# Padded pair scores, list flags on another engine, and an experts' first layer computed transposed, in an attention and mixture-of-experts kernel

## The chip, the cores and the metric

The kernel runs on one core of one Trainium2 chip. The metric is the device time of one execution in microseconds. Before the change it is 2405.32 us, the median of three runs (2403.5 to 2418.53). The profile was taken in an execution whose span, from the first to the last instruction, is 2203.7 us; positions in time below are microseconds from the start of that span.

## The reference, cut to what matters

One layer: graph attention over a sparse adjacency, then a mixture of 8 experts of which each token uses 2. There are 4096 tokens of 512 numbers, 8 heads of 64.

```python
def gnn(n, adj, Wks, Wqs, Wvs, Wo):
    adj = maximum(adj, eye)
    q, k, v = (einsum('nd,hdk->hnk', n, W) for W in (Wqs, Wks, Wvs))
    scores = einsum('hqk,hmk->hqm', q, k) * 64 ** -0.5
    scores = scores + 0.01 * eye - 1e16 * (1 - adj)
    return einsum('hqm,hmk,hko->qo', softmax(scores), v, Wo)

def ffn(x, Wg, bg, W1, b1, W2, b2):
    topk_scores, topk_idx = top_k(x @ Wg + bg, 2)
    h = gelu(einsum('nd,edh->neh', x, W1) + b1)      # 8 experts, 512 -> 512
    y = einsum('neh,ehf->nef', h, W2) + b2           # 512 -> 512
    return sum over the two chosen experts of softmax(topk_scores) * y

x = x + gnn(layernorm(x), adj, ...)
x = x + ffn(layernorm(x), ...)
```

The adjacency is 4096 x 4096 in float32, random, with many more entries among the first tokens than among the last.

## The kernel before

All matrix products are in float32; a float32 matmul is two records in the trace, a transpose is one. There are three stages.

**Stage one** (64 steps, in an order written by hand): keys, values and queries of all tokens are projected and stored in device memory. At the same time the adjacency is read in 32 pieces of 2 MB, one for each tile of 128 queries, and for each tile a list of the keys that any of its queries has is made. Keys that only the first 64 or only the last 64 queries of the tile need stand at the ends of the list, so that a chunk of 128 keys is "half" or full. Part of the making of lists is a comparison of slot numbers with the places at which each run of keys begins:

```python
def begun(i):
    for k, (t0, t1) in enumerate(ranges(i)):
        started[i, k] = lp.tile([P, (t1 - t0) * P], BF16, ...)
        nc.gpsimd.tensor_scalar(
            started[i, k], slots[:, t0 * P : t1 * P], base[g][:, k, j : j + 1], None,
            op0=ALU.is_ge)

def list_rows(i, k):                      # TensorE: started as weights, small matmuls
    ...
        nc.tensor.matmul(pr[:, t, :], started[i, q][:, s], row_x[g][:, r, j, :], ...)

load_at = {13 * i // 8: i for i in range(NT)}                       # step of each load
lists_from = {13 * (g * G + G - 1) // 8 + 3: g for g in range(NTB)}  # 4 tiles a group
...
    if u - 2 in load_at:
        neighbours(load_at[u - 2])        # VectorE: reduces a piece of the adjacency
```

**Attention**: for each tile of queries, its own 128 keys and then each chunk of its list (395 items in all; 229 of them are half, 166 full). An item's keys, values and mask are gathered from device memory by GpSimd. A step of the pipeline is:

```python
turn(n + 3)     # 8 transposes of 64-row blocks of the keys, 64 x 64, to PSUM pk
scores(n + 2)
values(n)       # 16 matmuls' records: weights 128 x 64 (values), 64 or 128 queries
later(n)        # pieces of the tile before: sums, rb, output product, routing
masked(n + 2)   # VectorE: e * mask

def scores(n):
    s = [ps_s.tile([P, NP, P], F32, ...) for r in range(2)]
    for p in range(NP):                   # 4 pairs of heads
        for r in range(2):                # the two heads of a pair, 64 rows each
            rows = slice(r * KD, (r + 1) * KD)
            nc.tensor.matmul(part(s[r], i, c)[:, p, :], k[rows, p, :],
                             q_in[i][rows, p, q], start=True, stop=True)
    for r in range(2):
        nc.scalar.activation(e[:, r * NP : (r + 1) * NP], part(s[r], i, c), AF.Exp)
```

Here `q` is 128 queries in a full item and 64 in a half one. During this stage the first layer's weights of all experts are loaded, 32 loads of 256 KB (`w1`). When it ends, the second layer's are loaded in 8 loads of 1 MB:

```python
w2 = w2p.tile([P, E, HC, D], F32, name="w2")
for e in range(E):
    nc.sync.dma_start(out=w2[:, e], in_=W2[e].rearrange("(c p) f -> p c f", p=P))
```

The routing writes each token's row, twice, to the place `xs_d` of its two experts, and a table says which expert and which place each of 71 tiles of 128 rows has.

**Experts**, 71 tiles, each with the weights of one expert:

```python
def turn(b):                              # 4 transposes of the rows to xT
def hidden(b):
    for c in range(DC):
        nc.tensor.matmul(ph, xTs[b][:, c, :], w1[:, bass.ds(es[b], 1), c, :], ...)
    nc.vector.tensor_add(h, ph, bs[b][:, 0])
    nc.scalar.activation(h, h, AF.Gelu)
def turn_hidden(b):                       # 4 transposes of h to PSUM pht
    ...
    nc.vector.tensor_copy(hT, pt)
def second(b):
    for c in range(HC):
        nc.tensor.matmul(py, hTs[b][:, c, :], w2[:, bass.ds(es[b], 1), c, :], ...)
    nc.vector.tensor_add(y, py, bs[b][:, 1])
    nc.scalar.mul(y, y, gate[:, 1:2])
    nc.gpsimd.indirect_dma_start(out=out, ..., in_=y, compute_op=ALU.add)

for b in range(NB):
    fetch(b + 4)                          # rows, b1 and b2 spread over 128 partitions
    turn_hidden(b); hidden(b + 1); turn(b + 2); second(b)
```

Of the kernel before, what the change touches and what calls it, by code (L numbers as in the profile page):

```python
# [20 lines left out]
P = 128  # L21
# [22 lines left out]
def kernel(  # L44
# [174 lines left out]
    def load_q(i):  # L219
        q_in[i] = qp.tile([P, NP, P], F32, tag="q", name=f"q_{i}")  # L220
        nc.sync.dma_start(out=q_in[i], in_=qT_d[:, :, ts(i, P)])
# [46 lines left out]
    with tc.tile_pool(name="wqkv", bufs=1) as wp, tc.tile_pool(name="p1", bufs=3) as work, tc.tile_pool(  # L268
# [39 lines left out]
        )  # L308

# [21 lines left out]
        def list_constants():  # L331
            nc.vector.tensor_sub(step, ident, step)
            nc.vector.tensor_mul(other, other, part)
            nc.vector.tensor_scalar(other, other, -1.0, 1.0, op0=ALU.mult, op1=ALU.add)
            nc.vector.memset(again_c, 1.0)
            nc.vector.memset(again_c[:, :, :, 0:1], 0.0)
            nc.vector.tensor_scalar_mul(corner, corner, -1.0)
            for k in range(KV // D):
                nc.sync.dma_start(out=kv_d[N : N + 1, ts(k, D)], in_=blank[:1, :D])
# [60 lines left out]
        def count_3(g):  # L400
# [24 lines left out]
            base[g] = b  # L425

        def steps(g):

# [3 lines left out]
            nc.tensor.matmul(  # L432
                pd[:, 1:], corner, x_g[:, :2], start=False, stop=True, skip_group_check=True
            )
            pe = ps_l.tile([P, G, NX], F32, tag="l", name=f"pe_{g}")
            nc.tensor.matmul(pe, step, x_g[:, 2], start=True, stop=True)
            dx = lp.tile([P, 4, G, NX], BF16, tag="dx", name=f"dx_{g}")
            nc.scalar.copy(dx[:, :3], pd)
            nc.scalar.copy(dx[:, 3], pe)
# [7 lines left out]
        def begun(i):  # L447

            g, j = divmod(i, G)
            for k, (t0, t1) in enumerate(ranges(i)):  # L450
                if t0 == t1:
# [5 lines left out]
                nc.gpsimd.tensor_scalar(  # L457
                    started[i, k], slots[:, t0 * P : t1 * P], base[g][:, k, j : j + 1], None,
                    op0=ALU.is_ge,
# [5 lines left out]
        def list_rows(i, k):  # L465
# [4 lines left out]
            for t in range(m):  # L470
                h = half_of(i, t0 + t)

                of = [(0, 0)] if h == 0 else [(2, 3)] if h == 1 else [(0, 0), (1, 1), (2, 2)]
# [8 lines left out]
        def list_keys(i, k):  # L482
# [21 lines left out]
            for h, u0, u1 in ((0, 0, a), (None, a, b), (1, b, listed[i])):  # L504
                u0, u1 = max(u0, t0), min(u1, t0 + m)
                if u0 < u1:
                    u = slice(at[i] + u0, at[i] + u1)
                    k = key[:, u0 - t0 : u1 - t0]
                    if h is None:
                        nc.vector.tensor_scalar_add(mask_of[:, u], k, float(i * (N + 1)))  # L510
                    else:
                        nc.vector.tensor_scalar(
# [27 lines left out]
        def lists_at(g, s):  # L540

            def rows(i):
                for k in range(len(chunks(i))):
                    list_rows(i, k)
                    if k:
                        list_keys(i, k - 1)
# [3 lines left out]
            if s == 0:  # L550
                count_1(g)
                return [lambda: count_2(g)]
            if s == 1:
                count_3(g)
                begun(i)
                return [lambda: steps(g)]
            if s == 2:
                begun(i + 1)
                return []
            if s == 3:  # L560
                return [lambda: rows(i)]
            if s == 4:
                keys(i)
                begun(i + 2)
                return [lambda: rows(i + 1)]
            if s == 5:
                keys(i + 1)
                begun(i + 3)
                return [lambda: rows(i + 2)]
            if s == 6:  # L570
                keys(i + 2)
                return [lambda: rows(i + 3)]
            keys(i + 3)
            return []
# [40 lines left out]
        def pack():  # L615
            i, c = ready.pop(0)
            m = work.tile([P, P], F32, tag="mask", bufs=6, name=f"pm_{i}_{c}")
# [5 lines left out]
        lists_from = {13 * (g * G + G - 1) // 8 + 3: g for g in range(NTB)}  # L623
        for u in range(8 * NTB + 1):
# [4 lines left out]
            for k in range(8):  # L629
                if u - k in lists_from:  # L630
                    due += lists_at(lists_from[u - k], k)
# [19 lines left out]
            if u - 2 in load_at:  # L651
                neighbours(load_at[u - 2])
                if load_at[u - 2] == NT - 1:
# [4 lines left out]
                    q_cm = tc.tile_pool(name="q", bufs=2, side="right")  # L658
                    qp = q_cm.__enter__()
                    load_q(0)  # L660
# [6 lines left out]
            if u - 8 in lists_from:  # L667
                g = lists_from[u - 8]
                ready += [
                    (i, c) for i in range(g * G, g * G + G) for c in range(listed[i])  # L670
                    if c % 5 in (1, 3)
                ]
# [29 lines left out]
    def route_1(m, l, pool, name):  # L702
# [4 lines left out]
        ahead = pool.tile([P, m, E, E], F32, tag="ahead", name=f"ahead_{name}")  # L707
        nc.vector.tensor_tensor(ahead, other, own, op=ALU.is_gt)
        same = pool.tile([P, m, E, E], F32, tag="same", name=f"same_{name}")
# [129 lines left out]
    w1_cm = tc.tile_pool(name="w1", bufs=1)  # L839
    w1p = w1_cm.__enter__()  # L840
    w1 = w1p.tile([P, E, DC, HID], F32, name="w1")
    GROUPS = [4] * (NT // 4 - 1) + [2, 1, 1]
    with tc.tile_pool(name="p2a", bufs=2) as two, tc.tile_pool(
# [38 lines left out]
        def load_x(i):  # L882
            x_in[i] = two.tile([P, D], F32, tag="xt", name=f"xr_{i}")
# [21 lines left out]
        def part(t, i, c):  # L905

            if half_of(i, c) is None:
                return t
            heads = t.shape[1]
            t = t.rearrange("p h q -> p (h q)")[:, : heads * QH]  # L910
            return t.rearrange("p (h q) -> p h q", h=heads)

        def scores(n):

            i, c = items[n]
            s = [ps_s.tile([P, NP, P], F32, tag="s", name=f"s{r}_{i}_{c}") for r in range(2)]
            k = kT.pop(n)
            q = queries(i, c)
            for p in range(NP):
                for r in range(2):  # L920
                    rows = slice(r * KD, (r + 1) * KD)
                    nc.tensor.matmul(  # L922
                        part(s[r], i, c)[:, p, :], k[rows, p, :], q_in[i][rows, p, q],
                        start=True, stop=True,
                    )
            if c < 0:
                e = two.tile([P, 2 * NP, P], F32, tag="acc", name=f"acc_{i}")
                acc[i] = e
            else:
                e = part(work.tile([P, 2 * NP, P], F32, tag="e", name=f"e_{i}_{c}"), i, c)  # L930
            for r in range(2):
                nc.scalar.activation(e[:, r * NP : (r + 1) * NP], part(s[r], i, c), AF.Exp)  # L932
            es[n] = e

# [8 lines left out]
        def values(n):  # L943
# [6 lines left out]
            for p in range(NP):  # L950
                for r in range(2):
                    h = 2 * p + r

                    nc.tensor.matmul(  # L954
                        po[i][r * KD : (r + 1) * KD, p, q], v[:, ts(h, KD)], e[:, r * NP + p, :],
                        start=(c < 0 and p == 0), stop=(c == listed[i] - 1),
                        skip_group_check=True,
                    )
# [10 lines left out]
        def piece(i, k):  # L969
# [3 lines left out]
            if k == 1:  # L973
                sums[i] = ps_e.tile([P, P], F32, tag="e", name=f"sums_{i}")
                a = acc.pop(i)
                for t in range(2):
                    for q in range(4):
# [3 lines left out]
                            a[:, r * NP + 2 * u + t, :], start=(t == 0), stop=(t == 1),  # L981
# [121 lines left out]
        loads = [(e, c) for e in range(E) for c in range(DC)]  # L1103
        for n, (i, c) in enumerate(items):
# [5 lines left out]
            if c == 2:  # L1110
                load_x(i)
            if n >= 56 and n % 7 == 0 and loads:
                e, d = loads.pop(0)
                nc.sync.dma_start(out=w1[:, e, d], in_=W1[e, ts(d, P), :])
            if c < 0 and i:
                osb[i - 1] = single.tile([P, NP, P], F32, tag="o", bufs=2, name=f"o_{i - 1}")
# [11 lines left out]
        osb[NT - 1] = single.tile([P, NP, P], F32, tag="o", bufs=2, name=f"o_{NT - 1}")  # L1128
        nc.scalar.copy(osb[NT - 1], po.pop(NT - 1))

# [3 lines left out]
        w2_cm = tc.tile_pool(name="w2", bufs=1, side="right")  # L1134
# [284 lines left out]
```

## Time and profile before

| what | value |
| --- | --- |
| time, median of 3 runs | 2405.32 us |
| span of the profiled execution | 2203.7 us |
| TensorE busy | 2040.5 us, 93% |
| VectorE busy | 1319.2 us, 60% |
| GpSimd busy | 1242.8 us, 56% |
| ScalarE busy | 870.1 us, 39% |
| moved by DMA | 481.71 MB, 219 GB/s over the span |
| mean granted TensorE clock | 0.949 of full |

In the profile, PE is the matmuls of TensorE and PEld its weight loads, DVE is VectorE, ACT ScalarE, POOL GpSimd and SP SyncE, whose queue issues most transfers. A group's line gives the line of the kernel, the engine, the operation, what it writes and reads, the count, and then the busy time and the mean duration of one in ns. The page cuts the span in 40 equal slices and prints one digit a slice: busy tenths for an engine, tenths of the full clock for PEclk, tenths of the 16 DMA engines' time for DMA. The timeline gives start, length, engine, line, operation and names; the ends of matmuls in it are modelled, while their starts are records. A wait is idle time of an engine just before an instruction, put down to what released it last.

### The profile page before, as it was taken

The numbers are of one execution on the slowest core, as the hardware profiler recorded it, in microseconds if no ns is written. First come the engines' busy times: TensorE is split into PE (matmuls) and PEld (weight loads), VectorE is DVE, ScalarE is ACT, GpSimd is POOL, SyncE is SP. The second block draws the span as 40 slices with busy tenths as digits, with TensorE's granted clock in tenths as the row PEclk, the third lists the DMA queues.
The fourth block names the chain that finished last, engine by engine and source line by source line (L and its number), as shares of the span: only waits on it lengthen the run. The fifth ranks groups of instructions, "written<-read, shape, count | busy, mean of one in ns | idle before, by whom it ended". The sixth has DMA issues, their size and how long they took to land. (4 is left out here: it accounts for less than half of the span.)

```text
span 2203.7 us, 52479 instructions
## 1 busy us (share of the span) xinstructions
PE 2040.5 (93%) x20620; PEld 1366.7 (62%) x20620; DVE 1319.2 (60%) x2387; ACT 870.1 (39%) x1842; POOL 1242.8 (56%) x1072
## 2 busy tenths in 40 slices
PE   7877879899999999999999999999829999999998
PEld 3333334348888888888788878777614444444444
DVE  4888586724887767777677777777723222333232
ACT  2121211124666646655556555656412222222222
POOL 1769888885888657678676766667412112111112
PEclk9988988896999989999999999999959999999999
DMA  7737787847788868878788878878475556555554
GB/s 281 301 127 234 258 294 261 263 120 236 247 260 273 273 216 275 281 239 282 247 268 266 267 249 248 264 234 252 165 257 127 134 131 136 136 134 140 137 136 96
DMA packets 215039, 481.71 MB, mean 219 GB/s; under 512 B 49618, under 2 KB 81874, under 8 KB 210692
## 3 DMA queue, kind: packets, MB, share of 16 engines
q0 software_dynamic: 79232, 242.18, 37.1%
q1 hardware_dynamic: 134404, 234.01, 33.7%
q8 instruction: 168, 2.75, 0.5%
q10 hardware_dynamic: 1152, 2.10, 0.3%
q14 instruction: 83, 0.68, 0.1%
HBM read 400.59 MB, written 77.58 MB: 217 GB/s over the span
## 5 line engine op out<-in xcount | busy, mean ns | idle before, releaser
L225 POOL DMA_INDIRECT kv<-kv_d,key_of x363 | 430.4, 1186 | 231.8 <-PE po L954 136.4
L941 DVE TENSOR_TENSOR e<-e,mask 128x512 f32<-128x512 f32 (+1 forms) x363 | 322.6, 889 | 204.0 <-ACT e L932 200.4
L922 PE MATMUL s<-q,kT 64*128 64x64 f32 (+1 forms) x5808 | 409.4, 282 | 2.7 <-ACT acc L932 2.7
L1354 POOL DMA_INDIRECT out_dram<-y,r x71 | 110.6, 1558 | 474.0 <-ACT h L1324 124.7
L922 PEld LDWEIGHTS s<-q,kT 64*128 64x128 f32 x5808 | 373.4, 196 | 2.9 <-ACT acc L932 2.9
L896 ACT COPY kT<-pk 128x512 f32<-128x512 f32 x395 | 232.1, 588 | 285.1 <-PE pk L893 277.3
L932 ACT ACTIVATE e<-s 128x256 f32<-128x256 f32 (+1 forms) x726 | 297.1, 461 | 101.5 <-PE s L922 98.6
L960 DVE TENSOR_TENSOR acc<-acc,e 128x512 f32<-128x512 f32 (+1 forms) x363 | 320.4, 883 | 1.4 <-PE po L954 1.4
L954 PE MATMUL po<-e,kv 128*64 128x64 f32 (+1 forms) x5808 | 311.3, 251 | 0.0
L225 POOL DMA_INDIRECT mask<-in_adjT_dram,mask_of x230 | 257.7, 1121 | 71.9 <-issue 50.0
L457 POOL TENSOR_SCALAR started<-slots,base 128x384 bf16<-128x384 int16 (+12 forms) x96 | 229.0, 2401 | 76.6 <-DVE longer L407 75.7
L954 PEld LDWEIGHTS po<-e,kv 128*64 128x64 f32 x5808 | 246.4, 141 | 34.7 <-issue 0.8
L1318 PE MATMUL ph<-w,xT 128*128 x568 | 258.3, 598 | 0.7 <-ACT xT L207 0.7
L1347 PE MATMUL py<-w,hT 128*128 x568 | 255.6, 593 | 0.9 <-DVE hT L1332 0.9
L352 DVE TENSOR_REDUCE flags<-adjT 128x64 f32<-128x4096 f32 x32 | 141.2, 4413 | 81.2 <-DMA adjT<-in_adjT_dram 81.2
L1352 DVE TENSOR_TENSOR y<-py,bb 128x512 f32<-128x512 f32 x71 | 49.1, 692 | 225.6 <-PE py L1347 184.2
L893 PE MATMUL pk<-ident,kv 64*128 64x64 f32 x2904 | 172.4, 240 | 11.4 <-ACT kT L896 11.0
L893 PEld LDWEIGHTS pk<-ident,kv 64*128 64x128 f32 x2904 | 122.0, 142 | 77.0 <-issue 47.2
L1318 PEld LDWEIGHTS ph<-w,xT 128*128 128x128 f32 x568 | 103.2, 192 | 104.1 <-issue 103.0
L1347 PEld LDWEIGHTS py<-w,hT 128*128 128x128 f32 x568 | 102.5, 190 | 104.0 <-issue 102.8
L225 POOL DMA_INDIRECT pm<-in_adjT_dram,mask_of x133 | 130.5, 981 | 41.5 <-issue 33.6
L1353 ACT ACTIVATE y<-y,gate 128x512 f32<-128x512 f32 x71 | 51.2, 722 | 213.1 <-DVE y L1352 213.1
(589 smaller groups left out, 2405.3 us busy)
## 6 DMA issues: line engine op xcount, KB each, us to landing
adjT<-in_adjT_dram SPq DMA_DIRECT2D x32, 2048.0 KB
bb<-in_L_ffn_b_dram SPq DMA_DIRECT2D x142, 256.0 KB
r<-xs_d SPq DMA_DIRECT2D x71, 258.0 KB
kv_d<-kv SPq DMA_DIRECT2D x32, 512.0 KB
xt<-in_x_dram SPq DMA_DIRECT2D x32, 256.0 KB
qT_d<-qT SPq DMA_DIRECT2D x8, 1024.0 KB
q<-qT_d SPq DMA_DIRECT2D x32, 256.0 KB
xr<-in_x_dram SPq DMA_DIRECT2D x32, 256.0 KB
```

The source lines that it names most:

```text
L225: nc.gpsimd.indirect_dma_start(out=to, out_offset=None, in_=src, in_offset=bass.IndirectOffsetOnAxis(ap=of[:, at[i] + c : at[i] + c + 1], ...
L352: nc.vector.tensor_reduce(flags[g][:, :, j, :], adj_in.pop(i).rearrange("p c (h q) -> p h c q", h=2), axis=AX.X, op=ALU.max,)
L457: nc.gpsimd.tensor_scalar(started[i, k], slots[:, t0 * P : t1 * P], base[g][:, k, j : j + 1], None, op0=ALU.is_ge,)
L893: nc.tensor.transpose(pk[:, r, ts(p, KD)], kv[n][half, ts(p, P)], ident[half, half])
L896: nc.scalar.copy(kT[n].rearrange("k p (r j) -> k r p j", r=2), pk[:, :, : NP * KD].rearrange("k r (p j) -> k r p j", p=NP),)
L922: nc.tensor.matmul(part(s[r], i, c)[:, p, :], k[rows, p, :], q_in[i][rows, p, q], start=True, stop=True,)
L932: nc.scalar.activation(e[:, r * NP : (r + 1) * NP], part(s[r], i, c), AF.Exp)
L941: nc.vector.tensor_mul(e, e, m.unsqueeze(1).to_broadcast(e.shape))
L954: nc.tensor.matmul(po[i][r * KD : (r + 1) * KD, p, q], v[:, ts(h, KD)], e[:, r * NP + p, :], start=(c < 0 and p == 0), stop=(c == listed[i ...
L960: nc.vector.tensor_add(acc[i][:, :, q], acc[i][:, :, q], e)
L1318: nc.tensor.matmul(ph, xTs[b][:, c, :], w1[:, bass.ds(es[b], 1), c, :], start=(c == 0), stop=(c == DC - 1),)
L1347: nc.tensor.matmul(py, hTs[b][:, c, :], w2[:, bass.ds(es[b], 1), c, :], start=(c == 0), stop=(c == HC - 1),)
```

## The change

The change has four parts. Stage one and attention are taken over from a sister of this kernel, the experts are new.

**Stage one.** The comparison with the slots becomes a sign of ScalarE (-1, 0 or 1 in place of 0 or 1; the steps that it selects are halved, and the rows at the edges are adjusted so that the sums come out the same). The scaling of the mask's row numbers goes from VectorE to GpSimd. Each piece of the adjacency is reduced three steps after its load is issued and not two, and the lists of a group begin one step later.

**Attention.** Queries are kept in two standing tiles with a zero block for the other head of each pair, so that a half item takes one matmul for two heads: all 128 rows, and 2 x 64 queries. A half item has one PSUM tile and one exponential, and a full one is computed as before. The order of heads in `e` becomes the plain one.

**Weights.** The second layer's weights are loaded during attention, in the same 32 loads of 256 KB; the first layer's are no longer kept. The 8 loads at the end of attention are gone.

**Experts.** Each tile loads its expert's first-layer weights, 1 MB, with its rows. The first layer is computed transposed, with blocks of these weights standing in TensorE and the rows' transpose moving, so that its result is already what the second layer needs. The bias goes into the activation, one column a partition, and the transposes of the hidden layer with their copy are gone.

```diff
-                nc.gpsimd.tensor_scalar(
-                    started[i, k], slots[:, t0 * P : t1 * P], base[g][:, k, j : j + 1], None,
-                    op0=ALU.is_ge,
-                )
+                nc.scalar.activation(
+                    started[i, k], slots[:, t0 * P : t1 * P], AF.Sign,
+                    bias=base[g][:, k, j : j + 1],
+                )
 ...
-        lists_from = {13 * (g * G + G - 1) // 8 + 3: g for g in range(NTB)}
+        lists_from = {13 * (g * G + G - 1) // 8 + 4: g for g in range(NTB)}
 ...
-            if u - 2 in load_at:
-                neighbours(load_at[u - 2])
+            if u - 3 in load_at:
+                neighbours(load_at[u - 3])
 ...
+                    q_two = [qp.tile([P, NP, 2, P], F32, name=f"q_{k}") for k in range(2)]
+                    (the block of the other head is set to zero, once)
 ...
+            if full:
+                (as before, from q_in[i][rows, p, r, :])
+            else:
+                s = ps_s.tile([P, NP, 2, QH], F32, tag="s", name=f"s_{i}_{c}")
+                for p in range(NP):
+                    nc.tensor.matmul(
+                        s[:, p], k[:, p, :], q_in[i][:, p, :, q], start=True, stop=True
+                    )
+                nc.scalar.activation(e, s.rearrange("p a r q -> p (a r) q"), AF.Exp)
 ...
-                nc.sync.dma_start(out=w1[:, e, d], in_=W1[e, ts(d, P), :])
+                nc.sync.dma_start(out=w2[:, e, d], in_=W2[e, ts(d, P), :])
 ...
-        for e in range(E):
-            nc.sync.dma_start(out=w2[:, e], in_=W2[e].rearrange("(c p) f -> p c f", p=P))
 ...
+            w1 = work.tile([P, DC, HID], F32, tag="w1", bufs=5, name=f"w1_{b}")
+            nc.sync.dma_start(
+                out=w1, in_=W1[bass.ds(e, 1)].rearrange("e (c p) h -> p (e c) h", p=P)
+            )
 ...
-            for c in range(DC):
-                nc.tensor.matmul(
-                    ph, xTs[b][:, c, :], w1[:, bass.ds(es[b], 1), c, :],
-                    start=(c == 0), stop=(c == DC - 1),
-                )
-            h = work.tile([P, HID], F32, tag="h", name=f"h_{b}")
-            nc.vector.tensor_add(h, ph, bs[b][:, 0])
-            nc.scalar.activation(h, h, AF.Gelu)
-            (turn_hidden: 4 transposes and a copy)
+            for m in range(HC):
+                for c in range(DC):
+                    nc.tensor.matmul(
+                        ph[:, m, :], w1s[b][:, c, ts(m, P)], xTs[b][:, c, :],
+                        start=(c == 0), stop=(c == DC - 1),
+                    )
+            for m in range(HC):
+                nc.scalar.activation(hT[:, m, :], ph[:, m, :], AF.Gelu, bias=bs[b][0][:, m : m + 1])
```

Beside these, some buffers become fewer to make room: masks being packed 5 for 6, the attention's `o` and `xr` tiles one for two, two temporaries of the routing one for two.

## The prediction

> **What bounds the kernel now.** I read the page first: its forty slices show three stages of different character, so every later view was asked by stage.
>
> ```profile
> PE   7877879899999999999999999999829999999998
> POOL 1769888885888657678676766667412112111112
> PEclk9988988896999989999999999999959999999999
> DMA  7737787847788868878788878878475556555554
> ```
>
> A slice is 55 us. Stage one (lists, projections) fills slices 1 to 9, to about 497 us: TensorE below full, GpSimd at eight or nine tenths, clock dips. Attention runs to 1590 us with TensorE at nine. The dent in slice 30 is the hand-over. Then the experts, again TensorE at nine, with a quiet GpSimd and DMA at half. The stages in numbers, from the windows view (busy us of each engine and count, then granted clock, DMA share, GB/s):
>
> ```profile
> 500.00:541.00 41.00, 38.30 (x436) 35.50 (x434) 15.97 (x36) 14.84 (x35) 21.34 (x22) 0.51 0.73 237
> 541.00:785.00 244.00, 243.31 (x4203) 208.03 (x4201) 192.25 (x250) 154.95 (x336) 183.84 (x150) 1.00 0.82 261
> 1650.00:2190.00 540.00, 540.00 (x1670) 266.07 (x1669) 164.24 (x347) 127.86 (x209) 107.54 (x69) 1.00 0.58 134
> ```
>
> Attention and experts are bound by TensorE: whatever VectorE, ScalarE or GpSimd save there is worth nothing by itself. But busy is a modelled union, so I price TensorE from the distance between the starts of successive groups, in its timeline:
>
> ```profile
> 924.03 0.69 PE L954 MATMUL po<-e,kv 128*64 128x64 f32 x16
> 924.65 1.16 PE L992 MATMUL rb<-rinv,spread 128*128 128x128 f32 x8
> 925.74 0.46 PE L893 MATMUL pk<-ident,kv 64*128 64x64 f32 x8
> ...
> 1203.39 0.46 PE L893 MATMUL pk<-ident,kv 64*128 64x64 f32 x8
> 1203.69 1.06 PE L922 MATMUL s<-q,kT 64*128 64x64 f32 x16
> 1204.68 0.69 PE L954 MATMUL po<-e,kv 128*64 128x64 f32 x16
> 1205.30 0.46 PE L893 MATMUL pk<-ident,kv 64*128 64x64 f32 x8
> ```
>
> A step on half of a tile's queries takes 1205.30 - 1203.39 = 1.91 us: transposes 0.30, scores 0.99, values 0.62. `rb` shows what eight records with a full 128x128 weight cost among other shapes: 1.09. At the start of attention the same things are slower, and one group ends that:
>
> ```profile
> 535.06 1.91 PE L922 MATMUL s<-q,kT 64*128 64x64 f32 x16
> 536.90 1.12 PE L954 MATMUL po<-e,kv 128*64 128x64 f32 x16
> 537.95 0.69 PE L893 MATMUL pk<-ident,kv 64*128 64x64 f32 x8
> 538.43 2.02 PE L922 MATMUL s<-q,kT 64*128 64x128 f32 x16
> 540.38 0.69 PE L954 MATMUL po<-e,kv 128*64 128x64 f32 x16
> 541.01 0.47 PE L893 MATMUL pk<-ident,kv 64*128 64x64 f32 x8
> ```
>
> Half steps run 3.37 us at half clock, one after another from 505 us on; within the first group of full scores (64x128) the clock comes back. It comes back in the step of the first full scores after the gaps at 786, 948, 1081 and 1562 us too. Half scores stream only 64 queries for a weight of 128 columns: TensorE keeps loading, and the clock does not rise.
>
> In stage one the waits decide (waiter, releaser, total, times, longest):
>
> ```profile
> DVE flags L352 <- DMA adjT<-in_adjT_dram: 81.2, 20, 10.6
> PE pr L476 <- POOL started L457: 31.9, 20, 3.2
> PE pt_a L206 <- ACT xn L200: 27.5, 7, 11.5
> PE pb L383 <- DVE x L377: 19.0, 5, 7.0
> ```
>
> **What the Trainium skill says.** (1) "TensorE: Matmul & The Clock Gate", Part 1: the clock is at half by default, and activity over some 3.4 us releases it. The trace agrees with half and with gaps of about 3 us bringing it on (clock 0.51 above), but shows that being busy is not enough: half steps stayed cold for 40 us. (2) Same page, LDWEIGHTS: a weight load costs by columns, not rows, columns/1.2 ns, so 107 ns for 128. Here pairs of 64-row scores start every 112 ns and `rb`'s full weights every 112 ns: it agrees. (3) "TensorEngine Tiling (Array Packing)", Key Properties: changing the tiling mode drains the array. Here a group of another shape starts 0.15 to 0.20 us after the last start of the one before, where one of the same shape starts after 0.06. (4) "SBUF — State Buffer", Terms: VectorE and GpSimd hold one port pair in turn, the loser fully blocked; ScalarE has its own. VectorE's casts of 128x14 numbers take 1436 ns in stage one and small operations elsewhere about 160, which fits it.
>
> **The change, part by part.**
>
> Stage one. 96 `started` comparisons (229 us of GpSimd, mean 2401 ns) become ScalarE's sign. ScalarE's copies of 512 and 256 columns take 586 and 383 ns, so 0.79 ns a column plus 0.18 us; some 2.7 us a tile against GpSimd's 7.2, about 80 us added to ScalarE's 105 in this stage. Not on the path, except where it delays a copy. Lists and neighbours start one step later, which gives each 2 MB adjacency load one step more. So the 32 us on `started` go; of `pt_a` and `pb` (46) I take half of what is not the start-up's 5, 20; fewer gaps also mean less half clock (44 us of full clock are lost in the stage): 15. Sum 67. Against it: the stage moves 119 MB and its DMA share summed by 50 us windows is 347 us of transfers. Ending at 430 would need a mean share of 0.81, which only the stage's best windows reach. I take two thirds: **-45**.
>
> Attention, half steps (3664 records / 16 = 229). Two 64-row matmuls of 64 queries become one of 128 rows and 128 columns on queries padded with zeros. 8 pairs x 112 ns become 8 records x 112 ns: nothing saved. But transposes and scores now differ in shape. From the last transpose to the last score it is 0.844 us now; `rb` behind half values takes 1.035 for the same course (drain 0.15, first pair of records 0.21, six more at 0.112). The step to the values stays 0.20. So +0.19 x 229 = **+44**, all on the bound. For it: 128 columns stream per weight, as in full scores, so the clock should recover in one step. Cold stretches now are 41, 20.5, 3.4, 10.2 and 10.2 us = 85, half lost; five of about 5 us would leave 25: (85-25)/2 = **-30**; I take 28. ScalarE's one exponential (595 ns) for two (2x383) and the freed bank are off the path. w2 for w1 in attention: the same 32 loads of 256 KB. Sum **+16**.
>
> The hand-over. The 8 MB of w2 go at 1590 to 1620 us; the DMA is full then, and the last scatters and `out` rows land late: VectorE waits 10.5 us for them before the table. That chain then has 8 blank rows to write anyway (issues 6.8 us, 5 more to the first read). I expect the first read 6 us earlier, but the first tile then waits for 1 MB of its own w1, about 4 us: **-3**.
>
> Experts, per tile now: 8 + 8 records of 512 columns at 429 ns = 6.87, 8 transposes at 109 = 0.87; 7.74 us. After: hidden 16 matmuls x 2 records x 112 = 3.57, second 3.44, one set of transposes 0.44: 7.45. x 71 = -21. Traffic: rows 258 KB, b2 256 KB, out 256 KB stay, b1's 256 KB go, w1's 1 MB comes: some 1.8 MB in 7.45 us = 245 GB/s, beside 134 now. The share 0.58 x 7.74 = 4.5 us becomes about 4.5 - 1.05 (b1 at 131 ns a packet of 2 KB, 128 packets over 16 engines) + 2.9 to 3.5 (512 packets at 91 to 110 ns; w2's took 91) = 6.4 to 7.0 of 7.45 us. It fits barely, with four tiles of lead; 4 us for stalls: **-17**.
>
> Sum -45 + 16 - 3 - 17 = -49: 2405 - 49 = 2356. The timed runs lie 200 us above the profiled span of 2204, which I take as a constant; if part of it is half clock, the padded scores recover more. For that I move to 2353.
>
> **Rivals.** (a) The experts become bound by DMA: for it, 0.9 of the engines' time; attention, however, holds 0.82 at 261 GB/s. If packets slow to 130 ns, a tile takes 7.7 and the gain there is gone: 2373. (b) Stage one is held by the adjacency loads, the longest wait in it (81 us on VectorE): then -15, in all 2385. (c) No drain penalty, the scores pair up as before: attention -28, in all 2310. (d) The clock stays cold in spite of the padding: attention +44, in all 2384. (e) Half clock is common in the timed runs: half steps at 3.37 for 1.91 us, 100 such are 146 us: below 2260.
>
> **Range and chances.** (a), (b) and (d) each cost 15 to 30 and seldom meet; (c) gains 45. 2305 to 2395 holds most pairs. The 2% line lies at 2357, just above my value: 0.54 faster, 0.41 same; slower by 48 needs (b), (d) and worse than (a) together: 0.05.
>
> **What would show it.** Stage one: the last projection at about 450 us, no TensorE wait on `started`. Attention: score groups of half steps about 1.09 us and a step about 2.1; the first cold stretch under 10 us. Hand-over: first `ph` near 1639 minus the gains before it. Experts: tiles 7.45 apart at clock 1.00, no wait of `ph` on w1, DMA share about 0.88. What would prove me wrong: weight loads not hidden behind 128 columns (tile above 8 us), ScalarE holding up the projections, or w1 arriving late.

## The result, and the profile after

The changed kernel takes **2342.8 us** (median of four runs, 2335.52 to 2353.84) where the kernel before takes 2408.3 (four runs, 2403.5 to 2418.53): a ratio of 0.973, 95% interval 0.967 to 0.978. It is faster by 2.7%. The prediction said 2353.

One circumstance is needed to read the numbers: the kernel before, unchanged, took 2199 us in one batch of runs and 2404 us in a later one on the same chip, so every ratio below is taken within its own batch, and the profile shown before the prediction (span 2203.7 us) is some 200 us shorter than the runs that were timed with it (2405 us).

So the kernel before was profiled again; `e1_before_again` below is that profile, with a span of 2406.9 us. The page's slices of it, the rows of TensorE, its clock and DMA (a slice is now 60 us):

```profile
PE   7787888889999999999999999999965999999998
PEclk9898899968789988998989999899987999999999
DMA  7746878556667766767677776666656655555665
```

And of the changed kernel, whose span is 2344.3 us (a slice is 58.6 us):

```profile
PE   7988887899999899989899998999939999999997
POOL 1044334666766565565555555566511111111121
PEclk9998998899999999999999999999969999999999
DMA  7778777667777777777787777777448988888885
```

Three things are to be seen. GpSimd fell in most of stage one (first eight slices) from eight and nine tenths, which the first profile showed, to three and four. The clock's sixes to eights in the slices of attention are gone. And DMA, at five or six tenths in the experts before, is at eight there now. The stages by the timeline (stage one ends with the copy of the last projection, attention with the last value product, the hand-over with the first `ph`; half clock is the sum of the stretches in which the granted clock was at half; one tile is the time from the first `ph` to the last matmul, divided by 71):

| us | stage one | attention | half clock in attention | hand-over | experts | one tile |
| --- | --- | --- | --- | --- | --- | --- |
| before, first profile | 497.1 | 1093.0 | 85 | 51.0 | 562.5 | 7.79 |
| before, profiled again | 496.5 | 1286.3 | 263 | 50.6 | 573.5 | 7.91 |
| after | 455.1 | 1250.5 | 99 | 50.5 | 588.3 | 8.15 |
| after minus before again | -41 | -36 | -164 | 0 | +15 | +0.24 |

The sum is -62, and the spans differ by 62.6. The total came out near the prediction, but not for its reasons: attention gave 52 us more than it was priced at, and the experts, which were to give 17, took 15. That 15 is uncertain: the old experts' code took 562.5 to 573.5 us in four profiles (the two above, 571.3 in `e1_old_experts`, 562.8 in `e3_before_wide`) and the new code 584.1 to 602.3 in four (588.3 above, 602.3 in `e1_old_scores`, 595.5 in `e2_wide_scores`, 584.1 in `e3_list_on_pool`), so the loss lies between 11 and 40 us.

### The profile page after: what moved, and what is told of

Read it like the earlier page. It is cut to its first block, busy times and chain, and to the rows that moved or that the text cites. A ratio compares the mean times of both kernels' runs of the same rounds, so it can differ in the third digit from the quotient of the medians.

```text
span 2344.3 us, 51509 instructions
## 1 busy us (share of the span) xinstructions
PE 2102.9 (90%) x20216; PEld 1519.5 (65%) x20216; DVE 1174.7 (50%) x2155; ACT 971.3 (41%) x1922; POOL 1027.9 (44%) x1080
## 5 line engine op out<-in xcount | busy, mean ns | idle before, releaser
L228 POOL DMA_INDIRECT kv<-kv_d,key_of x363 | 404.7, 1115 | 394.2 <-PE po L987 218.5
L987 PE MATMUL po<-e,kv 128*64 128x64 f32 (+1 forms) x5808 | 325.1, 251 | 18.6 <-issue 18.2
L1355 PEld LDWEIGHTS ph<-xT,w 128*128 128x128 f32 x2272 | 267.0, 195 | 85.6 <-issue 74.1
L228 POOL DMA_INDIRECT mask<-in_adjT_dram,mask_of x234 | 282.4, 1207 | 72.9 <-issue 61.6
L1355 PE MATMUL ph<-xT,w 128*128 128x128 f32 x2272 | 274.2, 280 | 38.5 <-DMA w<-in_L_ffn_W_dram 36.9
L964 PE MATMUL s<-q,kT 128*128 128x128 f32 x1832 | 281.6, 299 | 3.3 <-issue 3.1
L1381 DVE TENSOR_TENSOR y<-py,b 128x512 f32<-128x512 f32 x71 | 49.1, 692 | 445.1 <-PE py L1376 445.1
L964 PEld LDWEIGHTS s<-q,kT 128*128 128x128 f32 x1832 | 235.7, 201 | 20.6 <-issue 4.7
L957 ACT ACTIVATE e<-s 128x512 f32<-128x512 f32 x268 | 147.0, 597 | 69.5 <-PE s L952 29.2
L967 ACT ACTIVATE e<-s 128x512 f32<-128x512 f32 x229 | 137.8, 602 | 82.6 <-PE s L964 51.2
L1361 ACT ACTIVATE hT<-ph,b 128x128 f32<-128x128 f32 x284 | 81.2, 368 | 209.3 <-PE ph L1355 209.3
```

The source lines that it names most:

```text
L228: nc.gpsimd.indirect_dma_start(out=to, out_offset=None, in_=src, in_offset=bass.IndirectOffsetOnAxis(ap=of[:, at[i] + c : at[i] + c + 1], ...
L957: nc.scalar.activation(e.rearrange("p (a r) q -> p r a q", r=2)[:, r], s[r], AF.Exp)
L964: nc.tensor.matmul(s[:, p], k[:, p, :], q_in[i][:, p, :, q], start=True, stop=True)
L967: nc.scalar.activation(e, s.rearrange("p a r q -> p (a r) q"), AF.Exp)
L987: nc.tensor.matmul(po[i][r * KD : (r + 1) * KD, p, q], v[:, ts(h, KD)], e[:, h, :], start=(c < 0 and p == 0), stop=(c == listed[i] - 1), s ...
L1355: nc.tensor.matmul(ph[:, m, :], w1s[b][:, c, ts(m, P)], xTs[b][:, c, :], start=(c == 0), stop=(c == DC - 1),)
```

## The experiments

Every ratio is to the kernel before in the same batch. The kernels of one heading without a note were run in one batch, in which the kernel before takes, for the first heading, 2410.9 us.

### The parts undone one at a time

**The kernel before, unchanged**, for a profile that is as long as the timed runs (no edit).

> The kernel before, unchanged, for a second profile: its first was 200 us shorter than its timed runs. Theory A (ordinary executions of it are slowed by something that the first profile escaped): time about 2408 us, the profiled span within 1% of it, and in attention, where the first profile took 1093 us, TensorE shows some 200 us of added stalls or half clock. Theory B (a constant part outside the profile): the profiled span is again about 2204 us and the attention again about 1093 us.

Measured: 2413.2 us, ratio 1.002 (0.9995 to 1.004). Its stages are in the table above. Against the first profile nearly everything, 193 us, is added in attention. The windows view of that stage (busy us of PE, PEld, DVE, ACT and POOL with counts, then granted clock, DMA share, GB/s):

```profile
496.00:1783.00 1287.00, 1204.09 (x17246) 996.07 (x17246) 803.06 (x1260) 630.67 (x1438) 729.25 (x645) 0.90 0.69 214
```

The clock is 0.90 where the first profile had 0.96, and there are gaps of a kind that was rare in that profile. In the timeline of TensorE (start, length, idle time before it and its releaser):

```profile
761.04 0.45 PE L954 MATMUL po<-e,kv 128*64 128x64 f32 x8
761.80 0.35 PE L954 MATMUL po<-e,kv 128*64 128x64 f32 x4 [0.31 <-issue]
762.53 0.35 PE L954 MATMUL po<-e,kv 128*64 128x64 f32 x4 [0.38 <-issue]
763.27 0.46 PE L893 MATMUL pk<-ident,kv 64*128 64x64 f32 x8 [0.39 <-ACT kT L896]
```

One group of 16 records is torn into three; "issue" says that no wait which the profile shows held them. What the tearing costs can be estimated from the starts of the matmuls at full clock: how much longer each group, and the step to the next, takes than its like usually takes in the first profile and in the batch of 2199 us. In this attention stage that is some 109 us, against 16 in the first profile. Together with half of the added half clock, (263-85)/2 = 89, it makes 182 of the 193 us. The tears do not follow the fetching of instructions: 17% of the longer ones fall into one of the 137 instruction transfers of the busiest queue, and 14% of random moments do.

**The half items' scores as before**, all else changed:

```diff
-                s = ps_s.tile([P, NP, 2, QH], F32, ...)         # one matmul for two heads, zeros in q
+                s = [... for r in range(2)]                      # two of 64 rows, 64 queries each
+                    for r in range(2):
+                        nc.tensor.matmul(s[r][:, p, :], k[rows, p, :], q_in[i][rows, p, r, q], ...)
```

> The kernel after, with the half items' scores as before: two 64-row matmuls a pair, two exponentials; queries still in padded tiles. Theory A (TensorE's change of shape, as the prediction priced it: 0.19 us x 229 items = 44 us lost by the padding, 28 us gained in clock): about 2327 us, 16 faster than the kernel after. Theory B (ordinary executions are short of instructions or of clock in the half items, and padding halves the score records): 40 to 100 us slower than the kernel after, about 2385 to 2440 us, with more stalls inside TensorE's groups.

Measured: 2407.1 us, ratio 0.998 (0.996 to 1.000), so without this part nothing of the gain is left. Attention takes 1289.0 us with 249 us of half clock; stage one keeps its gain (454.2), and the experts give most of it back (602.3, 29 above the kernel before; 14 of these are more than the same code took in the changed kernel). In sum the torn groups cost about the same with and without the padding (113 us here, 108 in the changed kernel), so against this form the padding wins by the clock: (249-99)/2 = 75 for the 44 of the changed shape. But the tears move. Of the half items' score groups at full clock, 52 of 184 are torn by more than 0.15 us here, with 16 records each, and 4 of 208 in the changed kernel, with 8; there the loss stands around the value groups in their place.

**The experts and their loads as before**, all else changed (first layer with the rows standing, `w1` loaded in attention, `w2` in 8 loads at its end).

> The kernel after, with the experts and the loads of both layers' weights as before (w1 in attention, w2 at its end, hidden layer turned by transposes): only stage one and attention are changed. Theory A (as predicted, the new experts save 17 us and the hand-over 3): about 2363 us. Theory B (w1's loads bind the new experts, whose tiles lie 8.1 us apart in the profile after, where the old ones took 7.75): about 2320 us, so that the new experts lose 25 us and win the hand-over at most.

Measured: 2323.3 us, ratio 0.963 (0.956 to 0.970): 19.5 us below the changed kernel. Its tiles are 7.87 us apart, and its experts take 571.3 us for 588.3. The new experts cost time.

**One load of first-layer weights for all tiles.** This leaves out 70 of the 71 loads, so that all tiles use the first one's weights:

```diff
-            w1 = work.tile([P, DC, HID], F32, tag="w1", bufs=5, name=f"w1_{b}")
-            nc.sync.dma_start(out=w1, in_=W1[bass.ds(e, 1)]...)
+            if b == 0:
+                w1s[0] = work.tile(..., bufs=1); nc.sync.dma_start(out=w1s[0], ...)
```

> The kernel after, but w1 is loaded for the first tile alone and all 71 tiles use it: it leaves out 70 loads of 1 MB, and the result is that of one expert's first layer. Theory A (the 1 MB a tile binds the experts): no wait of ph on w1, tiles 7.45 us apart for 8.1, so about 46 us faster than the kernel after, 2297 us. Theory B (TensorE itself is slower with 128-column weights, or rows and b2 arrive late): tiles stay near 8 us and the time within 10 us of 2343.

Measured: 2294.5 us, ratio 0.950 (0.943 to 0.957); tiles 7.48 us apart, 7.44 from start to start in the middle of the stage. The windows view of 400 us among the experts, first of the changed kernel, then of this one:

```profile
1800.00:2200.00 400.00, 377.42 (x2172) 273.06 (x2171) 53.59 (x150) 115.42 (x295) 76.26 (x49) 0.99 0.86 226
```

```profile
1800.00:2200.00 400.00, 400.00 (x2373) 297.76 (x2372) 58.79 (x162) 125.29 (x321) 84.03 (x54) 1.00 0.54 107
```

Without the loads TensorE is busy throughout; with them it is idle for 23 of 400 us, at a DMA share of 0.86. The arithmetic of the new form is as cheap as priced, and the 1 MB a tile is what is paid for it: the experts take 540.5 us for 588.3.

### Other ways to have both gains

These four were run in the batch in which the kernel before takes 2198.9 us. The changed kernel was not run there as it is; the last of the four is nearly it.

**Both halves of the queries streamed in a half item**: 64-row pairs as before, but 128 queries for each weight, of which the exponential takes 64.

```diff
-                        s[:, p], k[:, p, :], q_in[i][:, p, :, q], start=True, stop=True
+                        s[r][:, p, :], k[rows, p, :], q_in[i][rows, p, r, :], ...
+                nc.scalar.activation(e..., s[r][:, :, q], AF.Exp)
```

> The kernel after, but a half item's scores are computed like a full item's: 64-row pairs that stream all 128 queries, of which only the 64 needed go through the exponential. No change of shape between transposes and scores, and more records than the padded form (16 for 8). Theory A (the padding wins because 128 queries stream for each weight and the clock rises again; its price is the drain of 0.19 us an item): the clock in attention is as in the kernel after (about 100 us of half clock, not 250), a half item's scores take 1.04 us for 1.09 and the transposes before it 0.30 for 0.39, so 229 x 0.14 = 32 us less: about 2311 us. Theory B (the padding wins because TensorE has fewer instructions to fetch): as with the old scores, about 2407 us.

Measured: 2198.2 us, ratio 1.001 (0.999 to 1.003). In this batch there is hardly half clock to lose (34 us of it here), so the two theories can't be told apart by the time; the next heading has the run that can. Its attention is 1091.2 us, 18 below the padded form's 1108.9 in the same batch. The whole gains nothing by it, since stage one took 6 us and the experts 10 us more than in that run. What the change of shape costs stands in the timelines. A half step of the changed kernel:

```profile
1199.46 0.46 PE L917 MATMUL pk<-ident,kv 64*128 64x64 f32 x8
1199.85 1.16 PE L964 MATMUL s<-q,kT 128*128 128x128 f32 x8
1200.94 0.69 PE L987 MATMUL po<-e,kv 128*64 128x64 f32 x16
1201.56 0.47 PE L917 MATMUL pk<-ident,kv 64*128 64x64 f32 x8
```

and of this kernel:

```profile
906.43 0.47 PE L917 MATMUL pk<-ident,kv 64*128 64x64 f32 x8
906.73 1.11 PE L948 MATMUL s<-q,kT 64*128 64x128 f32 x16
907.77 0.69 PE L975 MATMUL po<-e,kv 128*64 128x64 f32 x16
908.38 0.46 PE L917 MATMUL pk<-ident,kv 64*128 64x64 f32 x8
```

From `pk` to `pk` it is 2.10 us padded and 1.95 here, against 1.91 in the kernel before. The 128-row scores follow their transposes after 0.39 us, the 64-row ones after 0.30. 229 steps of 0.15 us are 34; 18 came: the wide kernel's TensorE is idle for 10 us more in this stage and at half clock for 7 us more.

**First-layer weights resident.** All experts' `w1` are loaded in attention, `w2` at its end, and VectorE copies each tile's 1 MB inside the chip to a standing buffer, two tiles ahead, so that the matmuls read their weights from a fixed place.

```diff
-            nc.sync.dma_start(out=w1, in_=W1[bass.ds(e, 1)].rearrange("e (c p) h -> p (e c) h", p=P))
+            w1s[b] = work.tile([P, DC, HID], F32, tag="w1s", name=f"w1s_{b}")
+            nc.vector.tensor_copy(w1s[b], w1[:, bass.ds(es[b], 1)].rearrange("p e c h -> p (e c) h"))
```

> The kernel after, but all experts' w1 are kept in SBUF as before (loaded in attention; w2 at its end), and VectorE copies a tile's 1 MB of w1 to a standing place, so that the hidden layer is still computed transposed. Theory A (the 1 MB a tile from device memory is what the new experts lose): tiles 7.48 us apart as with a single w1, about 46 us faster than the kernel after, 2297 us; the hand-over stays at 50 us. Theory B (the copy takes over 4 us or holds up GpSimd's adds): tiles 7.9 us or more, about 2325 us.

Measured: 2154.9 us, ratio 0.981 (0.976 to 0.986); tiles 7.485 us apart, the same as with one load for all. The hand-over, with the 8 MB of `w2` in it again, takes 51.5 us.

**Both of these together.**

> Both at once: streamed half scores and w1 copied from SBUF. If the two causes are independent, the sum of their gains: about 2265 us. If one of them alone fails, the time of the other.

Measured: **2139.0 us**, ratio 0.973 (0.969 to 0.978), 60 us under both the kernel before and the form nearest to the changed one. This is the best version found. It gains more than the two alone (44 and 1 us against that form), since the 18 us of the wide scores are no longer lost in the experts. In the list of its groups (busy time, mean ns, idle before and what ended it) the copy is:

```profile
L1336 DVE COPY w1s<-w 128x2048 f32 x71 | 87.1, 1228 | 126.8 <-PE ph L1350 119.9 <-SPq L1191 6.9
```

1.23 us of an engine that is idle for most of a tile, in place of a transfer of 1 MB. Its windows view among the experts has TensorE busy for all of 400 us at a DMA share of 0.55.

**One buffer more for the biases** (`b1` and `b2` 5 for 4), all else as changed.

> The kernel after with five buffers for b1 and b2, as the rows and w1 have, in place of four: the queue no longer waits for a tile's end before it can issue the w1 of the fourth tile ahead. Theory A (the DMA's rate binds the experts): within 8 us of the kernel after, 2335 to 2350 us, and ph waits on w1 as often. Theory B (w1 is late only because it is issued late): no waits on w1, up to 46 us faster, 2297 us.

Measured: 2199.1 us, ratio 1.000 (0.998 to 1.001); tiles 8.11 us apart, so these buffers are not what delays the loads. As the nearest thing to the changed kernel in this batch, it also shows that the change gains nothing here: stage one takes 46 us less than in the first profile, attention 16 more and the experts 23 more. This is its attention, with 27 us of half clock:

```profile
451.00:1560.00 1109.00, 1084.71 (x15401) 885.25 (x15403) 802.84 (x1258) 617.98 (x1208) 741.01 (x651) 0.99 0.80 247
```

### Single suspicions

The first three were run in a batch in which the kernel before takes 2404.4 us.

**The kernel before with wide half scores alone**:

```diff
-                        part(s[r], i, c)[:, p, :], k[rows, p, :], q_in[i][rows, p, q],
+                        s[r][:, p, :], k[rows, p, :], q_in[i][rows, p, :],
-                nc.scalar.activation(e[:, r * NP : (r + 1) * NP], part(s[r], i, c), AF.Exp)
+                nc.scalar.activation(e[:, r * NP : (r + 1) * NP], s[r][:, :, q], AF.Exp)
```

> The kernel before with one edit: a half item's pairs of heads stream all 128 queries, and the exponential takes the 64 needed. Nothing else changes. Where the kernel before takes about 2410 us its attention has 263 us of half clock; theory A (the clock) expects about 100 of these to stay, (263 - 100) / 2 = 80 us gained and 229 x 0.054 = 12 lost: ratio 0.97. Where the kernel before takes about 2200 us, with 85 us of half clock, theory A expects some 30 to stay: 28 gained, 12 lost, ratio 0.993. Theory B (the clock comes back for another reason than streaming): half clock as before and 12 us slower, ratio 1.005.

Measured: 2371.3 us, ratio 0.987 (0.982 to 0.992). Half clock in attention falls from 263 us to 75, by streaming more columns and nothing else. But only 35 us of time come back (1251.7 for 1286.3). 188 us at half clock are 94 of lost work, and the wider scores cost 12. The rest goes into tearing: by the estimate used above torn groups cost 153 us here and 109 in the kernel before, and 117 of 371 score groups are torn by more than 0.15 us. 94 - 12 - 44 = 38, near the 35 that came.

**The list flags on GpSimd as before**, with the later start of lists and neighbours kept:

```diff
-                nc.scalar.activation(started[i, k], slots[...], AF.Sign, bias=base[g][:, k, j : j + 1])
+                nc.gpsimd.tensor_scalar(started[i, k], slots[...], base[g][:, k, j : j + 1], None, op0=ALU.is_ge)
```

> The kernel after, with the comparison of the lists on GpSimd and its arithmetic as before; lists and neighbours still start one step later. Theory A (the waits of TensorE on the flags were the larger part of stage one's gain): stage one, which took 497 us before and 455 or 451 after, takes about 485, and the whole is some 30 us slower than the kernel after. Theory B (the later start alone gives the gain, GpSimd would have kept up): stage one within 8 us of 453.

Measured: 2428.1 us, ratio 1.011 (1.007 to 1.015). Stage one takes 537.3 us: 82 more than in the changed kernel, where 30 had been expected, and 41 more than in the kernel before. The list of waits in its first 500 us:

```profile
PEld L484 <- POOL started L465: 97.9, 46, 9.7
PE pr L484 <- POOL started L465: 89.6, 43, 9.5
```

In the kernel before the second of these waits is 32 to 39 us. With all else as changed, where the comparison runs is worth 82 us. That the stage is 41 us longer than before shows that the other edits alone (later start, lists made in another order, 25 us of mask scaling on GpSimd) make TensorE wait longer for GpSimd; which of them does it is not separated, and the comparison was not moved without them.

**All second-layer biases loaded once**, all else as changed (this takes 256 KB a tile off the DMA).

> The kernel after, with the second bias of all experts loaded once, spread over the partitions (16 KB each), and not 256 KB for every tile. Theory A (the new experts are bound by the sum of DMA work, of which b2's packets are about a seventh): 0.65 us a tile less, tiles 7.48 us apart for 8.13, no waits of ph on w1, 46 us faster than the kernel after. Theory B (w1's own loads are slow, whatever else moves): tiles above 7.9 us, under 16 us faster.

Measured: 2362.9 us, ratio 0.983 (0.979 to 0.987). DMA's share among the experts falls from 0.86 to 0.74, and yet the tiles are 8.33 us apart, not closer; the experts' 601.3 us lie within the 584 to 602 of the unchanged code. The tile's time is therefore not simply the sum of what DMA has to carry.

**More buffers in the experts** (rows 8 for 5, biases 8 for 4), in a batch with the kernel before at 2415.8 us:

```diff
-            r = work.tile([P, W], F32, tag="row", bufs=5, name=f"r_{b}")
+            r = work.tile([P, W], F32, tag="row", bufs=8, name=f"r_{b}")
```

> The kernel after with eight buffers for rows, b1 and b2 in the experts, in place of five, four and four; w1 keeps five. Theory A (a loop over five tiles binds the experts: the add of tile b-5 into the output must land before its row buffer can be filled for tile b, and the same queue issues w1 after that row; 7.6 us from that add's issue to the row's issue, 2.0 to w1's, 8.9 to ph, 22.5 to the tile's own add, 41 us in all, over 5 is 8.2 a tile): no wait of the queue on the adds, w1 there in time, tiles 7.5 to 7.7 us apart, the experts 545 us for 588. Theory B (the DMA engines, 0.86 of whose time was taken, give no more): tiles stay at 8.1, and ph waits on w1 as often.

Measured: 2343.3 us, ratio 0.972 (0.969 to 0.975), as the changed kernel. `ph` waits no more on its weights, but from 1800 to 2300 us another wait is there instead:

```profile
DVE y L1381 <- DMA out_dram<-y,r: 278.6, 43, 7.3
```

VectorE cannot write the next `y` until the adding of an older one into the output has landed. Tiles are 7.97 us apart at 226 GB/s and a share of 0.85, the changed kernel's 226 and 0.86. In the changed kernel, with 5 row buffers, a row's load waits for the add of five tiles ago, in the same 500 us:

```profile
SPq L1329 <- DMA out_dram<-y,r: 306.4, 62, 8.1
```

This wait alone is no proof, since it stands with one load for all tiles too (312.2 us in 490). But from the issue of an add to the issue of the row load that waited for it is 7.6 us in the changed kernel and 4.8 with one load: the adds land later beside the weights. The weights are issued 2.0 us after the row, and the tile's `ph` starts only 8.9 us after that, little more than one tile. With 8 row buffers these 8.9 are 18.2, the weights are there in time, and the late adds hold VectorE instead. Whether they land late because DMA has reached its rate or because each takes longer under load is open; more buffers for `y` as well were not tried.

## Why the prediction was right and wrong

**Stage one: right.** -45 was said, -41 came. TensorE's waits on `started` (32 us) are gone; in all it is idle for 63 us of the stage where it was for 91, and half clock falls from 75 to 44 us, the 15 us of lost work that were said. ScalarE's sign has a median of 934 ns, against the 0.9 us that the estimate gives (from a copy of 512 columns and, at 383 ns, an exponential of 256, which the prediction calls a copy). Rival (b), the adjacency as what holds the stage, falls: VectorE's wait for it stays, at 60 us for 81, and the gain came all the same. Rows of the waits of the changed kernel up to 455 us:

```profile
DVE flags L359 <- DMA adjT<-in_adjT_dram: 59.8, 14, 11.2
...
PE pt_a L206 <- ACT xn L200: 47.8, 13, 11.1
```

One term of the sum of 67 failed: `pt_a` waits longer than in the first profile (27.5), where 20 us of it and `pb` were to go. The cut to two thirds covered that. VectorE's slow casts, which the prediction read as a sign that it shares a port with GpSimd, fit this reading: the casts of `key_of` took up to 4.4 us before, take at most 0.4 after, and up to 2.7 where the comparison is back on GpSimd.

**Attention, the change of shape: right.** From the last transpose to the last score it is 0.844 us before and 1.036 after, the 0.19 that was read from `rb`; 229 times make the +44. Where half clock is rare in both, before to padded is 1093.0 to 1108.9 us: the +16 of the prediction. The mechanism cited from the Trainium skill, "TensorEngine Tiling (Array Packing)", Key Properties, that another tiling drains the array, fits these starts: the first score comes 0.153 us after the last transpose with a new shape and 0.059 with the same one. Rival (c), no penalty, falls; so does (d), since the first stretch of half clock in attention is about 14 us long (10 had been said) where it was over 40. A step of 2.10 us and scores of 1.09 are as said.

**Attention, the clock: the mechanism right, the term mis-sized.** The failed step is "(85-25)/2 = -30; I take 28". For a run as short as the first profile it holds: half clock goes from 85 us there to 27 in the batch of 2199 us, where 25 had been said. But the timed runs were 200 us longer, and the prediction took this difference "as a constant", which it is not: in runs of that length the kernel before has 263 us of half clock in attention and the changed one 99. Put in the same formula, (263-99)/2 = 82 for 28, and 44 - 82 = -38 for the +16; measured is -36. Rival (e), half clock common in the timed runs, was the right one in direction, though far from its 146 us. That the sum agrees does not show that the clock is all: the wide scores save 188 us of half clock without the +44 and end at the same place, 1252 us, because their groups are torn for 44 us more than the kernel before's, while the padded kernel's are not (108 for 109). So it looks like chance that the two come out equal. The windows views of the attention of the kernel before with wide scores and of the changed kernel:

```profile
499.00:1750.00 1251.00, 1154.67 (x17231) 934.24 (x17231) 800.73 (x1261) 629.70 (x1438) 730.23 (x644) 0.97 0.72 220
455.00:1706.00 1251.00, 1154.84 (x15415) 930.85 (x15415) 801.67 (x1259) 610.66 (x1210) 745.25 (x652) 0.96 0.74 219
```

In both TensorE is idle for 96 of 1251 us, against 24 of 1109 in the batch of 2199 us above, and DMA moves 219 and 220 GB/s for 247. What tears the groups apart in the longer runs, padded or wide (1246 to 1253 us in seven kernels), stays open.

**Hand-over: missed by little.** -3 was said, 0 came (50.6 to 50.5).

**Experts: wrong in sign.** TensorE was priced rightly: 7.45 us a tile said, 7.48 measured both with one load for all and with resident weights. So was the amount of DMA work: 0.86 of 8.15 us is 7.0 us a tile, where 6.4 to 7.0 had been said, and that is less than 7.45. The failed step is "It fits barely, with four tiles of lead; 4 us for stalls". The lead is not there: the weights are issued 8.9 us before they are used, because a row's buffer comes free, and with it the queue that also issues the weights, only when an add five tiles back has landed, 7.6 us after its own issue. Within 8.9 us the weights are often not complete. In the timeline:

```profile
1849.44 3.60 PE L1376 MATMUL py<-w,hT 128*128 x8
1854.37 3.81 PE L1355 MATMUL ph<-xT,w 128*128 128x128 f32 x32 [1.34 <-DMA w<-in_L_ffn_W_dram]
```

About half the tiles stand so: the list of waits has 36 of this one, 36.9 us in all, up to 5.0. The prediction named "w1 arriving late" as what would prove it wrong, and rival (a) gave the tile 7.7 us; it took 8.15. With a lead of 18.2 us the weights were in time and a tile still took 7.97, so what sets this time in the end stays open.

**The sum**: -41 - 36 + 0 + 15 = -62 for -49. Two errors of 52 and 32 us, of opposite sign, left 13: that the total came out near was luck.

## What to carry to other kernels

Before pricing a kernel from a profile, compare the profile's span with the timed runs: if they differ, find the stage in which they do, because the same term can be three times as large there. Where a TensorE-bound stage shows half clock, try to stream as many columns as the weights have, even columns that nobody uses, and prefer the same tile shape as the neighbours' (0.19 us a change here): that was the wide form, 18 us better than the padded one where the clock was not the trouble and as good where it was. For a load a tile from device memory, it is not enough that the bytes fit in the tile's time: ask what must happen before the load can be issued, and how long before its use that is (8.9 us here, where four tiles had been counted on). An otherwise idle engine's copy from resident weights (1.23 us for 1 MB) gave the whole of the arithmetic's gain.

## What the runs showed of the hardware that was not expected

In the first profile a TensorE that was busy for 35.97 of 36 us (505 to 541) stayed at half clock while half items followed one another, whose scores stream 64 columns for weights of 128. Streaming 128 for the same weights took half clock in attention from 263 us to 75. The Trainium skill, "TensorE: Matmul & The Clock Gate", Part 1, gives activity over some 3.4 us as what releases the clock; these runs show that the kind of activity matters. They do not give a clean rule: full values, which stream 128 columns for weights of 64, did not bring the clock back at 791.6 and 795.8 us of the first profile, while 9 of the 29 stretches of the second ended without a full score in their last 6.8 us.

One kernel, unchanged, took 2199 us in one batch and 2404 to 2416 in others, nearly all of the difference in attention, with groups of matmuls torn by gaps of 0.3 to 0.4 us that no semaphore explains. In the experts, loading 1 MB of weights a tile beside the adds made these land later (7.6 us for 4.8 from the issue of an add to the issue of the row load that waits for it); taking 256 KB a tile away lowered the DMA share from 0.86 to 0.74 and not the time.
